# Another order of score tiles, maxima and values in two attention layers

## The chip, the core and the metric

The kernel runs on one core of a Trainium2 chip. The metric is device time in microseconds: the median of three runs, 6107.12 us for the kernel before (6103.73 to 6114.92). One more execution was taken with the hardware profiler; all views below come from that one.

The engines are called by the names of the profile: PE is TensorE, with PEld for its loads of the stationary operand, DVE is VectorE, ACT is ScalarE, POOL is GpSimd, and SP is SyncE, which here only issues DMAs. PSUM is the memory that matmuls write to. [...]

## The reference, cut to what matters

Four layers follow each other. Each is an attention over a context and a feed-forward part, and each part gets the layer-normed tokens and adds its result to them. There are 1024 tokens and 6404 context rows, 128 wide. The two layers that the change touches (1 and 3) have 16 heads of 8 and a softmax over the keys:

```python
scores = jnp.einsum('bhqd,bhkd->bhqk', q, k) * HEAD_DIM ** (-0.5)
attn = jax.nn.softmax(scores, axis=-1)
out = jnp.einsum('bhqk,bhkd->bhqd', attn, v)
```

So for every head and query the kernel needs the largest score, the exponentials of score minus maximum, their products with the values, and their sum.

## The kernel before

`attn_softmax` computes one of these two layers. It works in 16 units. A unit is a pair of heads (p and p + 8, called g = 0 and 1) and one half of the queries (512). The 6404 keys make 51 blocks of 128, the last one short; a unit therefore has 102 score blocks (key block c, head g), each of 128 keys by 512 queries.

Three kinds of work are woven into one stream, and they are named by letters:

- **S** (lines 1205 to 1223) fills a score tile and takes its exponential. The two heads lie in the two 64-row halves of the array (33 rows each are used: eight numbers four times over, as high and low parts, and a row that brings in the negative maximum). Score tiles alternate in form. An x tile has two PSUM banks and takes two score blocks; a y tile has one bank and takes one. PE fills it (line 1218), and ACT writes the Exp to SBUF as px or py (line 1223). There is one x tile and one y tile in PSUM (lines 1069 and 1070); the SBUF tiles px and py have three buffers each.
- **M** (`more_max`, line 1091, and `max_group`, line 976) computes approximate scores for 128 queries and 512 keys in bf16, one matmul for each head (line 990), and DVE takes their maxima (line 994). The PSUM tile, `pair_ps`, has two buffers. 52 such groups belong to a unit, and they are those of the next unit: the maxima run 8 groups ahead of it. The last group of a unit is followed by `max_found` (line 1023) and two steps later by `max_to_rows` (line 1029), which transposes the maxima on PE and adds them into the query operand qS.
- **P** (`values`, line 1104) multiplies the exponentials of one pair of key blocks (four score blocks) with the values; four matmuls of 32 columns each stand side by side in the array (line 1108), and the result adds up in one PSUM bank, `o_ps`, over the unit.

The loop over the pairs of key blocks has 26 steps in a unit. What a step issues, and in which order, stands in a tuple of strings, and step i takes string i % 3; i begins at 0 in each unit:

```python
order = ("SMSMSP", "SMSMP", "SMSMSP")
```

From there `tc.manual_schedule` (line 1076) makes PE, ACT and DVE issue in exactly this order; each engine waits where an operand or a buffer isn't ready. P takes the pair of the step before (`waiting`, line 1231). S does nothing when the unit's 102 score blocks are gone, and M does nothing when all maxima of the layer are done. Behind each step line 1232 makes one more M if the maxima have fallen behind.

When P has worked off a unit's last pair, `finish` (line 1153) starts a chain: `out_of_banks` copies o_ps to `ob` on ACT and sends the denominators through DRAM to spread them; three steps later `inverted` inverts them on DVE; six steps later `normalized` brings them into all rows with a matmul (line 1140) and multiplies on DVE (line 1141); seven steps later `projected` multiplies with the output weights (line 1147) and adds to the tokens (line 1151); eight steps later the DMAs for the queries of unit u + 2, and the keys of pair p + 2, are issued (`loads`, line 1173). These jobs are put behind the step that is due, and those that need PSUM take a buffer of `pair_ps` in turn with M.

In unit 15 no maxima are left. The buffers of `pair_ps` are given back, and each M of the strings takes a piece of other work instead (lines 1202 and 1204): in layer 1 the keys of layer 2, and in both layers, from step 9 on, the first half of the experts.

## Time and profile before

| What | us |
|---|---|
| median of three runs | 6107.12 |
| the profiled execution | 6117.12 |
| its span (first to last instruction) | 6115.4 |
| layer 1's units (first values 1099.6, last output copy 2310.9) | 1211 |
| layer 3's units (first values 4785.6, last output copy 6007.0) | 1221 |
| one undisturbed unit (output copies at 1249.88 and 1320.32) | 70.44 |
| PE, DVE, ACT busy between 1500 and 1600 | 92.5, 85.5, 74.9 of 100 |

A line of a group names the source line, engine, operation, the tiles written and read, the shapes and the count; behind the first bar stand the busy time and the mean time of one in ns; behind the second the time the engine stood idle just before, and what released it. A line of the timeline has the start, the time it took, the engine and line, how many instructions were merged (x2), and in brackets the idle time before it with its releaser. A line of the waits names who waited for whom, with total, number and longest. A line of the windows has the stretch and its length, then the busy time and number of instructions of PE, PEld, DVE, ACT and POOL, then the granted clock of TensorE, the share of the DMA engines and GB/s. The starts of matmuls are exact; their ends are modelled, and they overlap in the array.

### The profile page before, as it was taken

The numbers are of one execution on the slowest core, as the hardware profiler recorded it, in microseconds if no ns is written. First come the engines' busy times: TensorE is split into PE (matmuls) and PEld (weight loads), VectorE is DVE, ScalarE is ACT, GpSimd is POOL, SyncE is SP. The second block draws the span as 40 slices with busy tenths as digits, with TensorE's granted clock in tenths as the row PEclk, the third lists the DMA queues.
The fourth block names the chain that finished last, engine by engine and source line by source line (L and its number), as shares of the span: only waits on it lengthen the run. The fifth ranks groups of instructions, "written<-read, shape, count | busy, mean of one in ns | idle before, by whom it ended". The sixth has DMA issues, their size and how long they took to land. (4 is left out here: it accounts for less than half of the span.)

```text
span 6115.4 us, 84274 instructions
## 1 busy us (share of the span) xinstructions
PE 5633.9 (92%) x33200; PEld 2168.9 (35%) x33408; DVE 4786.1 (78%) x5825; ACT 4225.9 (69%) x5284; POOL 965.7 (16%) x687
## 2 busy tenths in 40 slices
PE   6999988899999998999999988999997899999987
PEld 2333335333333345333333333333333333333334
DVE  5555535888888844999999899999998888888834
ACT  3555544677777775788888777788884677777764
POOL 4888883100000010000000000000002000000001
PEclk8999988899999998999999899999997899999978
DMA  0000011100111041000000000000002100011001
GB/s 18 3 2 3 1 48 51 31 14 14 16 18 17 4 151 44 13 13 14 13 14 14 11 11 11 11 15 13 15 10 65 33 14 14 14 16 19 7 16 40
DMA packets 139360, 130.46 MB, mean 21 GB/s; under 512 B 30749, under 2 KB 120277, under 8 KB 137982
## 3 DMA queue, kind: packets, MB, share of 16 engines
q1 hardware_dynamic: 129894, 103.35, 7.7%
q0 software_dynamic: 5296, 17.22, 0.9%
q8 instruction: 264, 4.33, 0.3%
q10 hardware_dynamic: 3760, 4.36, 0.2%
q14 instruction: 146, 1.20, 0.1%
HBM read 102.18 MB, written 35.85 MB: 23 GB/s over the span
## 5 line engine op out<-in xcount | busy, mean ns | idle before, releaser
L994 DVE TENSOR_REDUCE mx<-pair_ps 128x2 f32<-128x1024 f32 x1612 | 1810.2, 1176 | 249.5 <-PE pair_ps L990 228.6
L1223 ACT ACTIVATE px<-x_ps 128x1024 f32<-128x1024 f32 x1088 | 1114.4, 1024 | 313.1 <-PE x_ps L1218 306.5
L1612 DVE TENSOR_TENSOR e<-e,inv 128x1024 f32<-128x1024 f32 (+1 forms) x816 | 992.7, 1218 | 11.0 <-PE pair_ps L1452 0.9
L1108 PE MATMUL o_ps<-px,v 128*32 128x512 f32 x4352 | 905.4, 620 | 0.0
L1108 PE MATMUL o_ps<-py,v 128*32 128x512 f32 x2176 | 897.9, 618 | 0.0
L1461 ACT CAST lb<-pair_ps 128x1024 bf16<-128x1024 f32 (+1 forms) x714 | 720.5, 1009 | 250.8 <-PE pair_ps L1452 227.2
L990 PE MATMUL pair_ps<-kb,qz 64*128 64x512 bf16 (+1 forms) x3224 | 826.5, 386 | 54.0 <-DVE mx L994 37.6
L1223 ACT ACTIVATE py<-y_ps 128x512 f32<-128x512 f32 x1088 | 647.3, 595 | 326.2 <-PE y_ps L1218 320.6
L1555 ACT ACTIVATE e<-x_ps 128x1024 f32<-128x1024 f32 (+1 forms) x816 | 840.8, 1030 | 29.6 <-PE x_ps L1552 27.9
L1564 PE MATMUL s_ps<-e,ident 128*128 128x512 f32 (+1 forms) x1632 | 851.4, 604 | 0.4
L1218 PE MATMUL x_ps<-qS,kS 33*128 33x512 f32 x2176 | 713.9, 534 | 125.8 <-ACT px L1223 125.7
L400 POOL TENSOR_TENSOR acc<-acc,pt 128x1024 f32<-128x1024 f32 x256 | 602.3, 2353 | 65.3 <-ACT pt L389 51.0
L342 DVE TENSOR_REDUCE mx<-b_ps 128x2 f32<-128x1024 f32 (+1 forms) x306 | 341.2, 1115 | 345.2 <-PE b_ps L338 345.2
L1218 PE MATMUL y_ps<-qS,kS 33*128 33x512 f32 x1088 | 570.0, 524 | 7.3 <-ACT py L1223 7.3
L1620 PE MATMUL o_ps<-e,vz 128*32 128x256 f32 (+1 forms) x6528 | 537.0, 399 | 7.9 <-DVE e L1612 7.7
L1469 DVE TENSOR_TENSOR low<-lb,low 128x1024 bf16<-128x1024 bf16 (+1 forms) x714 | 487.1, 682 | 20.1 <-ACT lb L1461 20.0
L1552 PE MATMUL x_ps<-mneg,identb 128*128 128x512 bf16 x1424 | 453.4, 389 | 40.4 <-issue 32.8
L1548 PE MATMUL x_ps<-qS,kS 32*128 32x512 f32 x1632 | 478.4, 582 | 0.0
L389 ACT ACTIVATE pt<-x_ps,bias 128x1024 f32<-128x1024 f32 x288 | 305.6, 1111 | 213.9 <-PE x_ps L384 199.0
L1218 PEld LDWEIGHTS x_ps<-qS,kS 33*128 33x128 f32 x2176 | 286.2, 192 | 460.9 <-ACT px L1223 217.0
L990 PEld LDWEIGHTS <-qz 64*128 64x128 bf16 x3224 | 265.9, 95 | 340.5 <-issue 240.0
L1218 PEld LDWEIGHTS y_ps<-qS,kS 33*128 33x128 f32 x1088 | 207.2, 190 | 476.4 <-issue 242.1
(387 smaller groups left out, 6298.4 us busy)
## 6 DMA issues: line engine op xcount, KB each, us to landing
kS<-kst SPq DMA_DIRECT2D x400, 64.0 KB
kS<-kd SPq DMA_DIRECT2D x120, 200.1 KB
w<-in_L_ffn_w SPq DMA_DIRECT2D x48, 256.0 KB
kst<-kd POOLq DMA_DIRECT2D x24, 512.0 KB, 14.0
kd<-kh SPq DMA_DIRECT2D x12, 512.0 KB
kd<-k SPq DMA_DIRECT2D x12, 512.0 KB
qS<-qd SPq DMA_DIRECT2D x256, 16.0 KB
kb<-in_L_ffn_w SPq DMA_DIRECT2D x16, 256.0 KB
```

Of the source, the lines that this page charges most:

```text
L400: nc.gpsimd.tensor_tensor(accs[u][:n], first[:n], pt[:n], ALU.add)
L990: nc.tensor.matmul(m[:, g, :n], qzs[u][r, ts(t, P)], kb[r, at : at + n], start=True, stop=True,)
L994: nc.vector.tensor_reduce(mxs[u][:, t, b], m[:, :, :n], AX.X, ALU.max)
L1108: nc.tensor.matmul(o[32 * j : 32 * j + 32], v[:, c, ds(VW * h, 32)], pt, start=i == 0, stop=c + 2 >= NK,)
L1218: nc.tensor.matmul(s[:, k], kS[p % 2][r, ts(c, P)], qS[u % 2][r], start=True, stop=True,)
L1223: nc.scalar.activation(pt[:, : len(some)], s[:, : len(some)], AF.Exp)
L1461: nc.scalar.copy(t[:n], m[:n])
L1469: nc.vector.tensor_tensor(low[:n], t[:n], low[:n], ALU.min)
L1555: nc.scalar.activation(pair(i, k), s[:n], AF.Exp)
L1564: nc.tensor.matmul(firsts[i], self.ident[:n], es[i, h // 4][:n, h % 4], start=k == 0, stop=k == K - 1,)
L1612: nc.vector.tensor_tensor(e, e, r, ALU.mult)
L1620: nc.tensor.matmul(outs[half][32 * g : 32 * g + 32, cols], vz[i % 2][:n, ds(P * j + 32 * g, 32)], es[i, j][:n, g, cols], start=c == 0 and ...
```

## The change

One line changes. Layers 1 and 3 both use it. In a step, values now stand behind two filled score tiles and two sets of maxima in one string, behind three of each in the next, and behind two score tiles and one set of maxima in the third. The first string has one more score tile behind its values.

```diff
-            order = ("SMSMSP", "SMSMP", "SMSMSP")
+            order = ("MSMSPS", "MSMSMSP", "SMSP")
```

Over three steps both tuples have eight S, six M and three P. Everything else is the same: buffers, tiles, the jobs behind the steps and the steps they are due at. A unit's 26 steps are eight times the three strings and then the first two once more; these two have four M before and five after.

## The prediction

> **What bounds the kernel now.** I read the page's shares and slices first, then the groups, then the waits and the timeline of layer 1's steady stretch, last the granted clock of short windows. S stands for filling a score tile (line 1218; x holds two score blocks, y one), M for a set of maxima (lines 990, 994), P for a block of values (line 1108); "section" is what PE issues between two P. A step takes one turn of the loop over pairs of key blocks; three steps make a round.

> ```profile
> PE 5633.9 (92%) x33200; PEld 2168.9 (35%) x33408; DVE 4786.1 (78%) x5825; ACT 4225.9 (69%) x5284; POOL 965.7 (16%) x687
> ...
> L994 DVE TENSOR_REDUCE mx<-pair_ps 128x2 f32<-128x1024 f32 x1612 | 1810.2, 1176 | 249.5 <-PE pair_ps L990 228.6
> L1223 ACT ACTIVATE px<-x_ps 128x1024 f32<-128x1024 f32 x1088 | 1114.4, 1024 | 313.1 <-PE x_ps L1218 306.5
> ...
> L1223 ACT ACTIVATE py<-y_ps 128x512 f32<-128x512 f32 x1088 | 647.3, 595 | 326.2 <-PE y_ps L1218 320.6
> ```

> No engine is full in these layers: the Exps of ACT wait 306.5 and 320.6 us for scores, the maxima of DVE 228.6 us. The waits of 1300 to 2000 us (us in total, times, longest) show the circle, since PE waits for the same Exps:

> ```profile
> ACT py L1223 <- PE y_ps L1218: 101.1, 155, 4.0
> ACT px L1223 <- PE x_ps L1218: 84.9, 182, 1.4
> DVE mx L994 <- PE pair_ps L990: 71.2, 96, 1.6
> ...
> PE x_ps L1218 <- ACT px L1223: 38.6, 78, 0.7
> ```

> There is one x tile and one y tile in PSUM, so an x can be refilled only after its Exp. One section of the timeline on PE, then ACT beside it:

> ```profile
> 1511.63 0.51 PE L1218 MATMUL x_ps<-qS,kS 33*128 33x512 f32 x2
> 1511.98 0.39 PE L990 MATMUL pair_ps<-kb,qz 64*128 64x512 bf16 x2
> 1512.02 0.58 PE L1218 MATMUL y_ps<-qS,kS 33*128 33x512 f32 x1
> 1512.35 0.48 PE L990 MATMUL pair_ps<-kb,qz 64*128 64x512 bf16 x2
> 1513.32 0.51 PE L1218 MATMUL x_ps<-qS,kS 33*128 33x512 f32 x2 [0.48 <-ACT px L1223]
> 1513.75 0.62 PE L1108 MATMUL o_ps<-py,v 128*32 128x512 f32 x1
> ...
> 1514.75 0.49 PE L1218 MATMUL y_ps<-qS,kS 33*128 33x512 f32 x1
> ```
> ```profile
> 1512.24 1.02 ACT L1223 ACTIVATE px<-x_ps 128x1024 f32<-128x1024 f32 x1 [0.63 <-PE x_ps L1218]
> 1513.16 0.59 ACT L1223 ACTIVATE py<-y_ps 128x512 f32<-128x512 f32 x1
> 1513.92 1.02 ACT L1223 ACTIVATE px<-x_ps 128x1024 f32<-128x1024 f32 x1 [0.17 <-PE x_ps L1218]
> ```

> This section is S M S M S with an x at both ends. From x to x: 0.60 to the Exp, 1.02 of Exp, 0.06 to the refill, 1.68 us; PE has nothing it may issue in the meantime. The three sections take 2.12, 1.13 and 1.60 (the last waits 0.4 for py), the P 1.00 each (1513.75 to 1514.75, 0.996 unrounded): **7.83 a round**, as repeated starts show (reduces at 1499.84, 1507.68, 1515.51).

> **The change, part by part.** It adds and removes no instruction: a round keeps 8 S, 6 M, 3 P. The DMAs of a unit hang on step numbers, so on SP and POOL nothing is moved past anything; the qz that POOL writes is wanted a whole unit later.

> *The round.* The new sections are: first M x M y; second x M y M x M y; third x M y. No wait is taken away; the two x that must lie 1.68 apart now have M y M between them, and y M follows. Rows for one matmul deep work: y M x M, 1506.92 to 1508.04, four matmuls in one half of the array, 1.13 with 0.07 of waiting; so about 0.24 each.
> - Second: x at 0, x again at 1.68, M; y must wait for the y before: its Exp starts at 0.60+1.02-0.10 = 1.52 (the next Exp starts 0.10 before the recorded end of the one before) and ends at 2.12, so y at 2.17, and P 0.41 behind a y: 2.58.
> - Third: x M y, one matmul less than 1.13: 0.89. Its x wants the Exp of the x at 1.68, over at 3.31; the section starts at 3.58. Free.
> - First: M x M y: the four of 1.13 without the wait and with the shorter load first, 1.02. Its x wants an Exp over at 5.21, issued at 5.5 or later. Free. Its own Exp ends at 7.2, before the next second section at 7.48.
> - Sum: 2.58 + 0.89 + 1.02 + 2.99 = **7.48**, 0.35 less than 7.83.

> DVE must follow: a reduce starts 0.43 behind its M, the next 1.13 later (two took 2.35, 1.22 + 1.13), and an M waits for the reduce two before. Reduces start at 0.77, 1.90, 3.04, 4.35, 5.9, 7.02 and again at 8.25: six need 6.8 of 7.48. M five waits to 2.06 and was due at 2.03. Hidden, with 0.6 to spare; if the cover went, the round could not fall below 6.8 anyhow.

> *The end of a unit.* 26 steps are 8 rounds and two steps. The second of these has one score block left and becomes x M y M M P: the third M waits for the first's reduce (over at 1.99), P at 2.36, and the next unit's second M waits 0.47 for DVE. The two steps cost 2.02 + 3.36 + 0.47 = 5.85; before 3.11 + 1.87 = 4.98 (P starts 1173.35, 1175.21). +0.85.

> *Work hung on steps.* The denominators' matmul (line 1140: 1194.99 to 1196.04) and the projection (1147: 1198.27 to 1199.36) cost 1.16 and 1.08 now. Line 1140 comes at the end of a first step: before behind P, now behind x, inside the second section. Its slot in the two M buffers makes the fourth M wait for the product on DVE (0.69, 1.22 behind the matmul, over at 2.33) and the fifth for a reduce over at 3.46, so P comes at 4.06 instead of 2.58: 1.48. Projection 1.09. The transposed maxima (0.58 now): 0.58 to 0.95, taken 0.8. Together +0.55.

> [...]

> *Unit:* 8 x (-0.35) + 0.85 + 0.55 = **-1.4 us of 70.44** (output copies at 1249.88 and 1320.32). Bounds: the sections of 0.89 and 1.02 by their issue times alone would be 0.81 and 0.93, round 7.31, unit -2.8; with 0.1 more each, 7.68 and +0.2. I keep the middle, nearest to the measured 1.13.

> *The slots.* The two left-over steps have 5 M instead of 4, so a unit has 53 for 52 groups. The maxima run ahead and end in step 14 of unit 14 instead of 21, leaving eleven steps there with S and P alone. At full clock these take about 7.17 a round by the same chain (ACT sets it), and unit 14 would take 66 instead of 69.5. But the clock:

> ```profile
> 1405.40:1408.80 3.40, 2.92 (x17) 0.82 (x14) 2.35 (x2) 2.46 (x3) 0.00 (x0) 1.00 0.50 60
> 1408.80:1415.60 6.80, 6.80 (x29) 3.35 (x28) 3.73 (x4) 1.62 (x2) 0.00 (x0) 0.50 0.51 63
> ...
> 5840.60:5853.00 12.40, 10.21 (x64) 3.23 (x62) 0.81 (x2) 9.09 (x12) 0.00 (x0) 1.00 0.00 0
> 5853.00:5904.00 51.00, 47.90 (x154) 15.35 (x152) 7.62 (x32) 23.21 (x31) 3.54 (x3) 0.50 0.01 1
> ```

> In layer 3 the granted clock (first number behind the brackets) fell to 0.50 twelve us after the last M and stayed, rounds of 11.6 (P at 5856.1 and 5867.8). Some six of the eleven steps at that pace cost 6.5 x (11.6-7.2)/3 = 10 us: unit 14 becomes +6. [...]

> *Sum.* Per layer thirteen whole units -18, unit 0 (its first nine steps wait for keys) -1, unit 14 +6; unit 15, with expert work in place of M, 0: -13, both layers **-27**. The profiled execution took 6117.1 (span 6115.4) and becomes 6090; the median shown is 6107.1, ten lower, and becomes **6080**.

> **The rivals.**
> 1. *More:* the short round of 7.31 and the clock staying up in unit 14: 27 units x 1.4 + 20 = 58 more, 6022. For: issue times 0.35 and 0.04 between S, M and y. Against: the four matmuls' 1.13.
> 2. *No change:* the round is 7.6, by 0.06 in each of the sections that I could not read off. A unit then gains 0.4, both layers 11, and unit 14's tails take 12 back: 6108. For: such short sections do not occur in the trace. Against: the same walk gives 7.83 for the old order.
> 3. *Slower, by the clock:* the window before a fall at 1408.8 holds line 1140 and half a section's waiting. Now that matmul is followed by two waits inside one section of 4.06, longer than the 3.4 us before that fall. A fall costs 1.5 or 2.9 us (units of 71.95 and 73.36 against 70.44); nine units of both layers have one, 21 us in all. If nearly all 28 whole units fall, 19 more at 2.4 are +45: 6125. It decides from 11 more falls on (27/2.4).
> 4. *It does not do what it says:* the strings put two, three and two score tiles before P in a step, but one S stands behind P in the first step, so that between P lie 2, 4 and 2. The walk is of that order: 6080, as forecast.

> **How the numbers follow.** Forecast (6045 to 6094) 0.42; rival 1 0.22; rival 2 0.17; rival 3 0.19. About 0.2% (12 us) is what a measurement of this kernel can tell from no change: faster 0.64, same 0.17, slower 0.19. The range goes from rival 1's 6022 to 6130, past rival 3.

> **What would show it.** Reduces of equal place 7.48 apart; PE waiting for px once a round, in the second section alone; output copies 69 apart; maxima of a unit found ever earlier; clock 0.50 in the tail of unit 14 of both layers. Rounds of 7.83 or more, or waits of M for DVE in ordinary rounds, make it wrong; so do more than some twenty falls of the clock.

## The result, and the profile after

The changed kernel takes 6112.04 us (median of 22 runs, 6097.79 to 6124.68) against 6099.34 us for the kernel before on the same chip (22 runs, 6089.27 to 6121.13): a ratio of 1.0021, with a 95% interval of 1.0013 to 1.0028. It is 12.7 us slower, where 27 us less were forecast. The profiled execution took 6121.45 us, its span 6119.7, 4.3 us more than that of the kernel before.

The page of the changed kernel, the same groups as before:

```profile
PE 5651.8 (92%) x33408; PEld 2085.3 (34%) x33408; DVE 4800.3 (78%) x5825; ACT 4214.1 (69%) x5284; POOL 965.2 (16%) x687
...
L994 DVE TENSOR_REDUCE mx<-pair_ps 128x2 f32<-128x1024 f32 x1612 | 1827.6, 1177 | 173.5 <-PE pair_ps L990 152.8
L1223 ACT ACTIVATE px<-x_ps 128x1024 f32<-128x1024 f32 x1088 | 1113.7, 1024 | 595.6 <-PE x_ps L1218 592.9
...
L1223 ACT ACTIVATE py<-y_ps 128x512 f32<-128x512 f32 x1088 | 645.1, 593 | 53.2 <-PE y_ps L1218 42.4
```

The waits were moved, and a few got less. ACT now waits 592.9 us ahead of x tiles and 42.4 ahead of y tiles (306.5 and 320.6 before); DVE waits 152.8 us for maxima's scores in place of 228.6. The waits of 1300 to 2000 us say the same:

```profile
ACT px L1223 <- PE x_ps L1218: 171.7, 326, 4.1
...
DVE mx L994 <- PE pair_ps L990: 45.3, 105, 1.6
PE x_ps L1218 <- ACT px L1223: 30.1, 63, 0.7
PE pair_ps L990 <- DVE mx L994: 19.7, 35, 1.3
```

PE's wait for px is down from 38.6 us (78 times) to 30.1 (63 times). The second section of a round on PE, up to the P behind it:

```profile
1497.21 0.49 PE L1218 MATMUL x_ps<-qS,kS 33*128 33x512 f32 x2
1497.55 0.39 PE L990 MATMUL pair_ps<-kb,qz 64*128 64x512 bf16 x2
1497.59 0.58 PE L1218 MATMUL y_ps<-qS,kS 33*128 33x512 f32 x1
1498.05 0.39 PE L990 MATMUL pair_ps<-kb,qz 64*128 64x512 bf16 x2
1498.88 0.50 PE L1218 MATMUL x_ps<-qS,kS 33*128 33x512 f32 x2 [0.44 <-ACT px L1223]
1499.26 0.39 PE L990 MATMUL pair_ps<-kb,qz 64*128 64x512 bf16 x2
1499.37 0.49 PE L1218 MATMUL y_ps<-qS,kS 33*128 33x512 f32 x1
1499.79 0.62 PE L1108 MATMUL o_ps<-px,v 128*32 128x512 f32 x2
```

From x to x 1.67 us (1.68 forecast), to P 2.58 (2.58). Reduces of equal place start at 1495.64 and 1503.11, 7.47 apart. The round is what the forecast said, and a unit without disturbance takes 68.9 to 69.3 us. The time is lost elsewhere. The layers cut by output copies, in the two profiled executions (units 1 to 13 are thirteen units together):

| us, before / after | layer 1 | layer 3 |
|---|---|---|
| units 1 to 13 | 930.6 / 916.8 | 922.3 / 920.1 |
| unit 14 | 69.5 / 74.8 | 70.5 / 75.4 |
| unit 15 | 131.3 / 141.0 | 151.9 / 151.5 |
| time at half clock in units 1 to 13 | 34.1 / 34.1 | 13.7 / 41.0 |
| starts of such a fall, both layers | 9 before | 14 after |

A fall of the clock in unit 1 of the changed kernel, and the one in the tail of its unit 14, in windows (the first number behind the brackets is the granted clock):

```profile
1198.60:1202.00 3.40, 2.60 (x12) 0.81 (x12) 2.55 (x4) 2.52 (x3) 0.00 (x0) 1.00 0.01 2
1202.00:1205.40 3.40, 3.40 (x16) 1.68 (x16) 1.73 (x2) 0.72 (x2) 0.00 (x0) 0.51 0.02 5
...
2140.70:2150.90 10.20, 8.84 (x53) 2.92 (x53) 0.69 (x1) 8.31 (x12) 0.00 (x0) 1.00 0.00 0
2150.90:2171.40 20.50, 19.75 (x69) 4.82 (x69) 0.00 (x0) 10.68 (x15) 0.00 (x0) 0.50 0.00 1
```

All 14 falls in units 1 to 13 of the changed kernel start 18.6 to 19.9 us behind the unit's start (that is, the output copy of the unit before), behind line 1140 (2.8 to 4.1 us behind its start). All nine of the kernel before start 16.6 to 17.0 us behind it, behind the same line (0.9 to 1.5 us). The granted clock of both profiles is 1.00 or 0.50 and nothing else. All falls of one profile, 42 before and 51 after, begin within 0.01 us of a common grid of 3.413 us (1202.05, 1341.99 and 1481.94 after are 41 steps apart) and last 3.41, 6.83, 10.24 us and so on, but for the one in which the profile ends. This makes a sharp test: each unit has one grid point in such a stretch. Before, every grid point that lay at 16.6 to 17.0 us brought a fall (9 of 9), and none of the 17 at other places (15.0 to 18.4). After, every one at 18.6 to 19.3 did (12 of 12), 2 of the 13 at 19.6 to 20.0, and not the one at 20.6. Where the grid lies against a unit differs from unit to unit and from profile to profile (the first falls start at 63.98 us before and at 61.99 after, 1.99 us apart, which is no whole step); the new order has the wider place to be hit. How wide, the run e1_ends below shows, whose units 1 to 13 have the same strings: every grid point at 18.1 to 19.6 us brought a fall (12 of 12). That is 1.5 us, against at most 0.8 before (no fall at 16.45 and at 17.22). In the kernel before, 29 runs of one comparison go from 6084.8 us at a mean clock of 0.964 to 6118.1 at 0.956, with a correlation of -0.97, so the spread between executions is the clock's too. And the falls are not those of one profile: all 22 runs of the changed kernel have a mean clock of 0.949 to 0.955, below the 0.956 to 0.964 of those 29 (the tail of unit 14 counts in it too).

PE was mostly busy ahead of the two falls shown: 2.60 of the 3.40 us ahead of the one in unit 1, and 8.84 of the 10.20 us ahead of the one in the tail of unit 14.

### The profile page after: what moved, and what is told of

The parts are those of the page before. It is cut to its first block, busy times and chain, and to the rows that moved or that the text cites. A ratio compares the mean times of both kernels' runs of the same rounds, so it can differ in the third digit from the quotient of the medians.

```text
span 6119.7 us, 84478 instructions
## 1 busy us (share of the span) xinstructions
PE 5651.8 (92%) x33408; PEld 2085.3 (34%) x33408; DVE 4800.3 (78%) x5825; ACT 4214.1 (69%) x5284; POOL 965.2 (16%) x687
## 3 DMA queue, kind: packets, MB, share of 16 engines
q0 software_dynamic: 5296, 17.22, 0.9%
## 5 line engine op out<-in xcount | busy, mean ns | idle before, releaser
L994 DVE TENSOR_REDUCE mx<-pair_ps 128x2 f32<-128x1024 f32 x1612 | 1827.6, 1177 | 173.5 <-PE pair_ps L990 152.8
L1223 ACT ACTIVATE px<-x_ps 128x1024 f32<-128x1024 f32 x1088 | 1113.7, 1024 | 595.6 <-PE x_ps L1218 592.9
L1612 DVE TENSOR_TENSOR e<-e,inv 128x1024 f32<-128x1024 f32 (+1 forms) x816 | 992.8, 1218 | 11.0 <-PE pair_ps L1452 0.9
L1108 PE MATMUL o_ps<-px,v 128*32 128x512 f32 x4352 | 929.7, 636 | 0.0
L1108 PE MATMUL o_ps<-py,v 128*32 128x512 f32 x2176 | 920.7, 630 | 0.0
L990 PE MATMUL pair_ps<-kb,qz 64*128 64x512 bf16 (+1 forms) x3224 | 636.3, 385 | 100.8 <-DVE mx L994 80.5
L1223 ACT ACTIVATE py<-y_ps 128x512 f32<-128x512 f32 x1088 | 645.1, 593 | 53.2 <-PE y_ps L1218 42.4
L1218 PE MATMUL x_ps<-qS,kS 33*128 33x512 f32 x2176 | 586.1, 528 | 101.8 <-ACT px L1223 101.8
L1218 PE MATMUL y_ps<-qS,kS 33*128 33x512 f32 x1088 | 620.7, 570 | 3.9 <-ACT py L1223 3.8
L1552 PE MATMUL x_ps<-mneg,identb 128*128 128x512 bf16 x1632 | 501.3, 389 | 7.6 <-DVE mneg L1474 7.6
L1469 DVE TENSOR_TENSOR low<-lb,low 128x1024 bf16<-128x1024 bf16 (+1 forms) x714 | 487.1, 682 | 19.9 <-ACT lb L1461 19.7
L1218 PEld LDWEIGHTS x_ps<-qS,kS 33*128 33x128 f32 x2176 | 217.6, 191 | 643.2 <-ACT px L1223 511.0
L990 PEld LDWEIGHTS <-qz 64*128 64x128 bf16 x3224 | 176.9, 94 | 640.6 <-issue 587.6
L1452 PE MATMUL pair_ps<-qn,kb 32*128 32x512 bf16 (+1 forms) x1632 | 319.5, 388 | 44.0 <-ACT lb L1461 21.2
```

Source lines behind the costliest of these rows:

```text
L990: nc.tensor.matmul(m[:, g, :n], qzs[u][r, ts(t, P)], kb[r, at : at + n], start=True, stop=True,)
L994: nc.vector.tensor_reduce(mxs[u][:, t, b], m[:, :, :n], AX.X, ALU.max)
L1108: nc.tensor.matmul(o[32 * j : 32 * j + 32], v[:, c, ds(VW * h, 32)], pt, start=i == 0, stop=c + 2 >= NK,)
L1218: nc.tensor.matmul(s[:, k], kS[p % 2][r, ts(c, P)], qS[u % 2][r], start=True, stop=True,)
L1223: nc.scalar.activation(pt[:, : len(some)], s[:, : len(some)], AF.Exp)
L1552: nc.tensor.matmul(s[:, t], self.identb, mnegs[i], start=False, stop=True)
```

## The experiments

Theory A: the short round is real; what takes it back are the falls at line 1140, the 53rd slot for maxima (line 1091's groups run ahead, and unit 14 ends in steps without them) and the two units at the ends. Rivals: the falls alone (B); or the order is slower on ordinary executions, whatever the profile shows (C). Each ratio is against the kernel before on the same chip. "Falls" are those in units 1 to 13 of the profiled execution: us at half clock in layers 1 and 3, and how far behind the unit's start they begin.

| kernel | us | ratio (95%) | falls | where |
|---|---|---|---|---|
| before | | 1 | 34.1, 13.7 | 16.6 to 17.0 |
| changed | 6112.0 | 1.0021 (1.0013 to 1.0028) | 34.1, 41.0 | 18.6 to 19.9 |
| e1_ends | 6106.7 | 1.0004 (0.9992 to 1.0017) | 37.5, 30.7 | 18.1 to 19.9, one at 10.2 |
| e2_slots | 6089.0 | 0.9983 (0.9968 to 0.9998) | 34.1, 64.9 | 17.4 to 20.8, five at 10.5 to 11.0 |
| e3_late | 6097.6 | 0.9991 (0.9979 to 1.0002) | 6.8, 20.5 | 19.5 to 19.8, one at 10.6 |
| e4_all | 6026.1 | 0.9868 (0.9851 to 0.9886) | 6.8, 0 | 11.5 |
| e5_slots_late | 6054.1 | 0.9914 (0.9896 to 0.9932) | 34.1, 13.7 | 10.5 to 11.6 |
| e6_rows | 6074.6 | 0.9947 (0.9929 to 0.9965) | 6.8, 0 | 10.7 |
| e7_before_late | 6085.9 | 0.9964 (0.9950 to 0.9978) | 0, 0 | |
| e8_nine | 6119.0 | 1.0018 (1.0006 to 1.0029) | 30.7, 30.7 | 25.8 to 27.0, one at 11.1 |
| e9_before_rows | 6072.7 | 0.9961 (0.9946 to 0.9976) | 0, 0 | |
| e10_slots_rows | 6042.4 | 0.9911 (0.9895 to 0.9927) | 0, 27.3 | 10.8 to 11.3 |
| e11_first | 6038.4 | 0.9907 (0.9890 to 0.9923) | 6.8, 0 | 11.9 |
| e12_last | 6047.3 | 0.9921 (0.9907 to 0.9936) | 20.5, 0 | 10.7, 11.0, 20.3 |
| e13_rows_last | 6073.3 | 0.9953 (0.9936 to 0.9971) | 0, 0 | |
| e14_slots_rows_last | 6049.4 | 0.9906 (0.9882 to 0.9930) | 13.7, 34.1 | 10.3 to 10.7 |
| e15_slots_rows_ends | 6030.6 | 0.9885 (0.9866 to 0.9905) | 6.8, 6.8 | 11.5, 12.0 |
| e16_slots_rows_again | 6037.9 | 0.9890 (0.9869 to 0.9910) | 27.3, 13.7 | 10.4 to 11.5 |
| e17_second | 6037.9 | 0.9880 (0.9860 to 0.9901) | 13.7, 10.2 | 19.4 to 21.5 |
| e18_all_second | 6025.3 | 0.9867 (0.9845 to 0.9890) | 10.2, 20.5 | 19.4 to 21.7 |

### One cause each, and all together

**Old strings in units 0 and 15** (e1_ends):

```diff
+            usual = ("SMSMSP", "SMSMP", "SMSMSP")
-                    for what in order[i % 3]:
+                    strings = usual if u in (0, UNITS - 1) else order
+                    for what in strings[i % 3]:
```

> Units 0 and 15 of both layers go back to the old strings, units 1 to 14 keep the new ones. Theory A (the loss sits in places of its own, besides the units that run evenly): in the profiled pair unit 0 lost 3.5 and 4.1 us and unit 15 of layer 1 lost 9.7 us, so this run should be some 17 us below the changed kernel, 6095 us or 0.999 of the kernel before. Theory B (the loss is the clock's falls at line 1140 in units 1 to 13 alone, which this leaves as they are): no gain, 1.002 of the kernel before. Theory C (the shorter round of the profile isn't there on ordinary executions, and the new order is the slower one wherever it stands): two of sixteen units go back, so at most 2 us of the 13 come back, 1.0015 to 1.002.

1.0004: 10 us come back, between A and B. With this interval and that of the changed kernel it is clear of none of the three.

**52 slots** (e2_slots):

```diff
-                    for what in order[i % 3]:
+                    for what in "MSMSP" if i == STEPS - 1 else order[i % 3]:
```

> Step 25 gets its own string MSMSP, so that a unit has 52 slots for maxima, not 53: the surplus no longer runs ahead, the steps around a unit's end lose one M, and the steps without maxima at the end of unit 14 become fewer. Theory A: 0.85 us at 28 unit ends is 24 us less, and the ends of unit 14, which lost 5.3 and 4.9 us in the profiled pair, give these back: some 34 us below the changed kernel, 6078 us or 0.9965 of the kernel before. Theory B (the clock's falls at line 1140 decide; what a unit's end saves in work is taken back by more falls): 6105 to 6112 us, 1.001 to 1.002. Theory C (order slower everywhere): 1.002.

0.9983: 23 us below the changed kernel, where A said 34. Units without a fall went from 69.2 to 68.0 us and unit 14 from 74.8 and 75.4 to 70.4 and 68.4, as forecast; but the falls of layer 3 rose from 41.0 to 64.9 us in the profiled execution. A is the nearer; of B it has that falls take back a part.

**Line 1140 a step later** (e3_late):

```diff
-                for i, f in ((3, second), (6, third), (7, fourth)):
+                for i, f in ((3, second), (7, third), (8, fourth)):
-                later.setdefault(at + 8, []).append(loads)
+                later.setdefault(at + 9, []).append(loads)
```

> Line 1140 comes one step later (7 steps after a unit's end), line 1147 8 steps after, the loads 9 steps after; nothing else is changed, so that the two-row matmul no longer stands in the stalled section where the changed kernel's clock falls to a half. Theory A: the falls in units 1 to 13 cost 19 us and 22 us in the profiled execution (15 and 6 before the change); without them 20 to 41 us less than the changed kernel, 6071 to 6092 us, 0.9955 to 0.999 of the kernel before, and a granted clock of 1.00 through units 1 to 13. Theory B (the same, and the only cause): at the lower end, 0.9955. Theory C (order slower everywhere, the falls are by the way): 1.001 to 1.002, falls or not. A rival to A within it (the clock falls wherever few rows stand, whichever step it is): the falls stay as many and move a step, 1.001 to 1.003.

0.9991, at A's upper end, and the falls went from 75.1 us to 27.3. Line 1140 now stands directly behind P, but behind the P of the section that waits 0.44 us for px, much as it stood in the kernel before (behind a wait of 0.48). All three falls left at this line start there, on neighbouring grid points (19.55, 19.66 and 19.77 us; none at 19.48 and 19.97). The profiled execution is the kernel's quickest (6084 of 6084 to 6120) and has a mean clock of 0.957, where the twelve runs go from 0.949 to 0.957, so others probably had more falls.

**The three together** (e4_all):

> The three edits together: old strings in units 0 and 15, 52 slots for maxima in units 1 to 14, line 1140 a step later. Theory A (three separate places, their prices add up): 17 + 34 + 20 to 41 us below the changed kernel, 6020 to 6041 us, 0.987 to 0.9905 of the kernel before. Theory B (only the clock at line 1140 counts): 0.9955 to 0.997. Theory C (order slower everywhere): 1.000 to 1.002.

0.9868, 77 us less than the kernel before beside it (6102.7) and A's lowest figure. It gives more than its parts (0.0017 + 0.0038 + 0.0030 below the changed kernel, against 0.0153): I read it so that falls take back what a shorter unit saves as long as they are there, as the rise in e2_slots suggests; no run isolates it. Theories B and C are out. Its page:

```profile
PE 5561.0 (92%) x33200; PEld 2080.5 (35%) x33408; DVE 4800.2 (80%) x5825; ACT 4206.8 (70%) x5284; POOL 965.7 (16%) x687
...
L994 DVE TENSOR_REDUCE mx<-pair_ps 128x2 f32<-128x1024 f32 x1612 | 1827.5, 1177 | 154.5 <-PE pair_ps L990 129.6
L1226 ACT ACTIVATE px<-x_ps 128x1024 f32<-128x1024 f32 x1088 | 1114.5, 1024 | 528.7 <-PE x_ps L1221 518.1
```

DVE is busy as long as in the changed kernel (4800). PE is busy 73 us less than in the kernel before (5633.9, with as many records): the same work, less of it at half clock (mean granted clock 0.961 and 0.956 in the two profiles).

### What it is about line 1140

**The same later place in the kernel before** (e7_before_late, the edit of e3_late):

> The kernel before with line 1140 a step later and nothing else. It has 52 slots already. Theory A (line 1140's place brings the falls in both orders): the falls of its units 1 to 13, 34 us and 14 us long and some 21 us in cost, go, and it runs at 0.9965 to 0.998. The round's own worth is then the distance from this kernel to the one with 52 slots and the later line 1140: by units of 70.45 and 68.0 us, 28 of them, 69 us or 0.011. Rival (the later place is only good for the new order, whose stalled section it was in): 0.999 to 1.001, or slower by new falls.

0.9964, no falls. So the kernel before paid for line 1140 too. The line now stands behind the P of its section without a wait. (The edit moves line 1147 and the loads as well; the runs with 128 rows below move nothing.) The other half of the expectation failed: from here to e5_slots_late, the new order with 52 slots and the later line, it is 0.0050 (30 us) and not 0.011; e5 still has 47.8 us of falls.

**Two steps more, in the same string again** (e8_nine):

```diff
+                for i, f in ((3, second), (9, third), (10, fourth)):
+                later.setdefault(at + 11, []).append(loads)
```

> The changed kernel with line 1140 9 steps after a unit's end in place of 6, line 1147 10 after, the loads 11 after: later than the kernel with 7, but back in the same string of the three, behind P and x. Theory A (it is the section that line 1140 stands in): the falls in units 1 to 13 stay, 30 to 45 us a layer, and the time at 1.001 to 1.003 of the kernel before. Rival (what helps is more distance from the unit's end and from its transfers): as the kernel with 7 or better, 0.998 to 0.9995, with falls of under 20 us a layer.

1.0018, falls of 30.7 us a layer, and they moved with the line: 25.8 to 27.0 us behind the unit's start, one round later than in the changed kernel. It is the section, not the distance. (In it unit 15's first half of the experts begins on tokens that lack unit 14's projection.)

**128 rows in place of 2** (e6_rows):

```diff
-                nc.tensor.matmul(m, sel, rr, start=True, stop=True)
+                nc.tensor.matmul(m, self.ident, ob, start=True, stop=True)
```

> The changed kernel with line 1140's matmul on 128 rows (identity by ob, the same 128 x 512 output in float32) in place of 2 rows; this leaves out the division by the sums. The same time on the engine, the same place in the same section, the same wait behind it. Theory A (few rows in a stalled section bring the clock down): the falls in units 1 to 13, 34 and 41 us long in the profile of the changed kernel, go to under 15 us a layer, and the time to 0.996 to 0.999 of the kernel before. Rival (the stall itself, with VectorE's answer behind line 1140, brings it down, whatever the rows): the falls stay, 1.001 to 1.003.

0.9947, 45 us less than the changed kernel, and none of the 26 grid points at 17.8 to 21.0 us brought a fall. The section itself is the same. First the changed kernel's, then this one's, with PE's matmul of line 1140 and the two M that wait behind it:

```profile
1198.43 1.12 PE L1140 MATMUL pair_ps<-rr,selr 2*128 2x512 f32 x2
...
1200.39 0.39 PE L990 MATMUL pair_ps<-kb,qz 64*128 64x512 bf16 x2 [0.29 <-DVE ob L1141]
...
1201.52 0.39 PE L990 MATMUL pair_ps<-kb,qz 64*128 64x512 bf16 x2 [0.51 <-DVE mx L994]
```
```profile
1890.76 1.13 PE L1140 MATMUL pair_ps<-ob,ident 128*128 128x512 f32 x2
...
1892.72 0.39 PE L990 MATMUL pair_ps<-kb,qz 64*128 64x512 bf16 x2 [0.29 <-DVE ob L1141]
...
1893.85 0.39 PE L990 MATMUL pair_ps<-kb,qz 64*128 64x512 bf16 x2 [0.50 <-DVE mx L994]
```

The windows of the second, at the same place against the grid as 1198.60 to 1202.00 above (18.9 and 19.1 us behind the unit's start):

```profile
1890.70:1894.10 3.40, 2.61 (x14) 0.99 (x12) 2.53 (x4) 2.27 (x3) 0.00 (x0) 1.00 0.00 0
1894.10:1897.50 3.40, 3.40 (x28) 1.64 (x29) 2.88 (x4) 1.38 (x3) 0.00 (x0) 1.00 0.00 0
```

One more thing differs, and it is not the clock. Behind the last unit of a layer line 1140 waits for the denominators' DMA (rr from rd, 14.5 us in all in the changed kernel), and the matmul on `ob` waits for none. From the last output copy of layers 1 and 3 to the end of the projection it is 15.5 and 21.0 us in the changed kernel and 9.5 and 15.8 here. So some 11 of the 45 us come from there and some 34 are left; units 1 to 13 of the two profiles differ by 33.

**The same 128 rows in the kernel before** (e9_before_rows):

> The kernel before with line 1140 on 128 rows (identity by ob), as in the changed kernel's version with 128 rows; the division by the sums is left out. The two then differ in the order alone, with the falls at line 1140 out of both. Theory A: its falls in units 1 to 13 go (21 us in cost), 0.9955 to 0.9975 of the kernel before; the changed kernel's version, at 0.9947, is below it by what the units give (26 units at 1.3 us, 34 us) less what the ends of unit 14 and unit 15 take (10 to 25 us): a distance of 10 to 25 us, 0.0015 to 0.004. Rival (128 rows only help the new order; the order before loses nothing at line 1140): 0.999 to 1.001.

0.9961, no falls: with 128 rows the kernel before gains 24 us (15 to 33 by the interval), and the changed one 45 us (34 to 57). Here too some 11 us are those of the layers' ends (17.3 and 23.9 us become 11.2 and 18.7); units 1 to 13 of the two profiles differ by 20, and e7_before_late, which keeps that wait, gained 23. With line 1140's rows out of both the new order leads by 0.0014 only, a little under A's range. Units 1 to 13 of this kernel take 915.8 and 916.7 us.

### The 53rd slot, and unit 0 and unit 15

**52 slots and a later line 1140, new strings everywhere** (e5_slots_late, the edits of e2_slots and e3_late):

> The 52 slots and the later line 1140, with the new strings in units 0 and 15 too. What is asked is whether those two units lose anything of their own. Theory A2 (they don't: what looked like a loss in unit 15 was the clock coming down out of unit 14, and unit 0 differs between runs of one kernel as much as between the two orders): as the version with all three edits, 6020 to 6035 us, 0.987 to 0.989 of the kernel before. Rival (the old strings are better in those units, by 3.5, 4.1 and 9.7 us as the profiled pair had it): 17 us above the version with all three, 6043 us, 0.9895 to 0.991.

0.9914, above the figures of both, though the rival's lie in its interval; falls of 34.1 us in layer 1, at a new place.

**128 rows and 52 slots** (e10_slots_rows):

> The changed kernel with 52 slots and with line 1140 on 128 rows in its own place (the division by the sums is left out). With 52 slots and two rows the falls of units 1 to 13 were more than ever (34 and 65 us long). Theory A (they are line 1140's): under 15 us a layer and 0.987 to 0.990 of the kernel before. Rival (a shorter unit brings the clock down by itself, through less work in each 3.4 us): falls of over 30 us a layer stay, 0.9955 to 0.9985.

0.9911, between the two; no fall at line 1140, but four at 10.8 to 11.3 us in layer 3.

**Old strings in one of the two units** (e11_first and e12_last, with the edits of e5_slots_late):

> 52 slots, later line 1140, old strings in unit 0 alone (unit 15 has the new ones). The version with the old strings in both units ran at 0.9868, the one with the new ones in both at 0.9914, and their profiles differ by 18 us in units 1 to 13 (falls of 7 and 0 us against 34 and 14 us) and by 9 us in the two units 15. Theory P (unit 0's string sets where the following units stand against the clock's steps of 3.41 us, of which 20 make 68.27 us, close to a unit's 68.0, so that a fall comes back unit after unit or never): falls of units 1 to 13 under 15 us a layer, 0.988 to 0.9895. Rival (it is unit 15's string): 0.9905 to 0.992.

> 52 slots, later line 1140, old strings in unit 15 alone (unit 0 has the new ones). Theory P (unit 0's string sets the falls of units 1 to 13, unit 15's gives 9 us in the two layers): falls of units 1 to 13 as with the new strings in both, 14 to 35 us a layer, and 0.989 to 0.9905. Rival (it is unit 15's string): 0.9865 to 0.988.

0.9907 and 0.9921. The falls went as theory P has it in layer 1 (one with the old strings in unit 0, three without); in layer 3 neither has any. The times did not: e11 lies in its rival's range, e12 above both of its own. Theory P is not shown.

**With line 1140's falls out** (e13_rows_last, e14_slots_rows_last, e15_slots_rows_ends, e16_slots_rows_again, together on one chip):

> The changed kernel with line 1140 on 128 rows (the division by the sums is left out) and the old strings in unit 15; 53 slots. Theory U (unit 15's new strings cost some 5 us in layer 1 and up to 13 in layer 3, by the profiles of the two versions with 128 rows: 136.9 and 151.5 us against 131.7 and 138.5): 10 to 18 us below the version with new strings everywhere (0.9947): 0.9918 to 0.9931. Rival (unit 15 is long because the clock comes down in the tail of unit 14, before it, whatever its strings): 0.994 to 0.9955.

> 128 rows, 52 slots, old strings in unit 15. Theory U: 6 to 15 us below the version with 52 slots and new strings everywhere that runs beside it. Rival (the tail of unit 14, which 52 slots take away): within 4 us of it.

> 128 rows, 52 slots, old strings in units 0 and 15. Theory P (unit 0's string only moves the units against the clock's steps, which matters only through line 1140's two rows): within 4 us of the version with the old strings in unit 15 alone. Rival (unit 0's string is worth something of its own, by the 3 to 4 us of the first comparison of profiles, in each layer): 6 to 8 us below it.

> 128 rows, 52 slots, new strings everywhere, beside the other three as their base: 0.9895 to 0.9927 of the kernel before, as the first time.

e13, at 0.9953, is where the rival has it; e14 is 11.5 us above e16 and fits neither; e16, at 0.9890, is a little under its range, and the same kernel had 0.9911 on another chip (e10). e13 to e16 is the slot alone but for unit 15: 6073.3 to 6037.9, 35 us, where 24 at units' ends and 10 in the tails were expected. Unit 15's strings alone (e13 against e6, e14 against e16) make no difference that these runs can tell. The profiles can: unit 15 of layer 1 takes 128.7 to 133.0 us in the ten with the old strings there and 133.4 to 141.0 in the ten with the new ones (means 130.9 and 135.7); with 52 slots as with 53; in layer 3 the means are 145.8 and 149.6, and the two groups overlap. Unit 0 ends at the same time with either (means 1178.8 and 1179.2 us in layer 1). e15 is 19 us below e14, neither "within 4" nor the rival's 6 to 8: the units of 68.0 us still have falls, 13.6 us of them in the profile of e15 and 47.8 in that of e14. That unit 0 decides how many is not shown.

### A second place

In e14_slots_rows_last the falls lie 10.3 to 10.7 us behind the unit's start. There stands the inversion of the denominators (lines 1130 and 1131), put behind step 3. DVE and PE of one such section, then its windows:

```profile
5313.21 0.17 DVE L1130 TENSOR_TENSOR dr<-dr 128x8 f32<-128x8 f32 x1 [0.63 <-DMA dr<-dd]
5313.41 0.20 DVE L1131 RECIPROCAL dr<-dr 128x8 f32<-128x8 f32 x1
```
```profile
5313.46 0.49 PE L1221 MATMUL x_ps<-qS,kS 33*128 33x512 f32 x2 [0.44 <-ACT px L1226]
5314.76 0.61 PE L990 MATMUL pair_ps<-kb,qz 64*128 64x512 bf16 x2 [0.80 <-DVE mx L994]
```
```profile
5311.30:5314.70 3.40, 2.22 (x17) 0.76 (x10) 2.73 (x6) 2.87 (x5) 0.00 (x0) 1.00 0.04 4
5314.70:5321.50 6.80, 6.74 (x28) 1.65 (x27) 3.49 (x4) 2.50 (x4) 0.00 (x0) 0.50 0.66 87
```

DVE waits 0.63 us for the denominators' DMA, the reduce behind it is late, and M waits 0.80 in the section that has waited 0.44 for px already. So the job was put a step later:

```diff
-                for i, f in ((3, second), (7, third), (8, fourth)):
+                for i, f in ((4, second), (7, third), (8, fourth)):
```

> 52 slots, line 1140 a step later (7), and the inversion of the denominators a step later too (4 in place of 3); new strings in all units. Theory S (the falls 10.3 to 12.0 us behind a unit's output copy are those of the inversion's wait for its DMA in the stalled section): no falls there, under 7 us of falls a layer in units 1 to 13, and 0.986 to 0.9885 of the kernel before, against 0.9914 without this edit. Rival (a unit of 68.0 us has falls somewhere whatever stands there): 14 us or more a layer, 0.990 to 0.992.

> The same with the old strings in units 0 and 15, the version that ran at 0.9868 with the inversion at 3. Theory S with P (unit 0's string matters only by which units meet a fall): within 6 us of the version beside it, whose units have no falls left to be moved. Rival (the old strings are worth something in these two units): 10 us or more below it. Against 0.9868 little is left to gain: 0.985 to 0.9875.

e17: 0.9880 against 0.9914, and none of 26 grid points at 9.8 to 12.9 us brings a fall. So the place is shown by the falls: in e5_slots_late, with the inversion a step earlier, seven start there. By the times it is not, since the intervals of e17 and e5 overlap. Under 7 us of falls a layer were expected, and 13.7 and 10.2 are left, now at line 1140's later place. e18 is at 0.9867 with 30.7 us of falls, 12.6 us below e17 as the rival has it, with intervals that overlap; in the two profiles 6 us of that are unit 15. e4 and e18 are the quickest versions, 1.3% below the kernel before.

## Why the prediction was wrong, point by point

1. **The round, right.** 7.47 to 7.48 us measured. P stand 3.58, 1.89 and 2.01 us apart (3.58, 1.89 and 2.02 from the sections). Rivals 1 and 2 are out. The 35 waits of M for the maxima's buffer between 1300 and 2000 all stand at work hung on steps or at a unit's end, none in an ordinary round. There is some luck in the two short sections: the 0.24 for a matmul is not a quarter of 1.13 less 0.07 (0.265), and they came out to 0.01 all the same.
2. **The unit, right.** With the clock held up, thirteen units take 899.8 and 900.4 us with the new order (e13) and 915.8 and 916.7 with the old (e9): -32.3 in both layers, against -36 from -1.4 a unit. The +0.85 at a unit's end has the right sign and about the right size: without the 53rd slot a unit takes 68.0 us in place of 69.2. In the changed kernel P follows the one before by 5.05 us where line 1140 stands (4.06 + 1.00 forecast).
3. **The step that failed: work hung on steps.** "Line 1140 ... now behind x, inside the second section" was priced at 1.48 us of waiting and no more. The waiting was right (point 2); the clock was left to rival 3, and the forecast took the falls of before as they were. The runs with 128 rows gain 24 us in the kernel before and 45 us in the changed one. Some 11 us of each arise at the layers' ends, where a DMA is no longer waited for, so that the falls cost some 13 and 34 us (20 and 37 in units 1 to 13 of the profiles, against e9 and e13). Some +21 us belonged into the sum, known to about 15 by the intervals; the profiles say +16. Rival 3 had the line and the place. Its measure was wrong: it let the forecast turn from 11 more falls on, and five more (14 against 9), at the greater length, were enough together with unit 15 (point 5).
4. **The slots, right.** Unit 14 +5.3 and +4.9 us against +6, from the clock in its tail, which fell 14.7 and 14.9 us behind the start of the last M. Rival 1's 20 us, for a clock that stays up there, no run shows: in the changed kernel 0.50 was granted for 20.5 us of that tail in both layers (from 2150.95 and from 5840.76). The surplus is worth more without it than the prediction could use: 35 us for a string of five letters.
5. **Unit 15, wrong: 0** against +4.8 us in layer 1 and about +4 in layer 3 (means of the profiles; the times of e13 and e14 don't show it). Here other work takes the letters' places, and I had walked only the stream of S, M and P. Which wait in unit 15 makes the difference was not taken apart.
6. **Unit 0, right within its size:** -1 against 0 (its end in layer 1, 1178.8 and 1179.2 us).

From the measured sizes: -32 + 21 + 10 + 9 = +8 us; 12.7 were measured. Some 5 stay unassigned, less than the +21 can be off by.

## What to carry to other kernels

A matmul can cost more than its duration. Line 1140 took 1.1 us here, with 2 rows as with 128, and with 2 rows the falls behind it cost some 13 us in the kernel before and 34 us in the changed one (point 3): look where such a line stands. Here the clock fell where it stood in a section that waits (0.29 and 0.51 us, the changed kernel) or behind one (0.48 in the kernel before, 0.44 for what is left in e3), and not where it stood behind a section without a wait (e7). Compare the granted clock of short windows at every line that a reordering moves. When a shorter loop gives less than its walk says, look for time at half clock before doubting the walk; here the same reordering comes to +0.2%, or with three small edits around it to -1.3%. Of that 0.4% is the later line 1140, which the kernel before could have had without the new order (e7).

## What the runs showed that I had not expected

- Two stretches with equal busy time (2.60 and 2.61 of 3.40 us) and equal waits, with line 1140 (1.1 us) on 2 rows in one and on 128 in the other, were followed by a granted clock of 0.51 and 1.00.
- Whether a fall comes is a matter of at most 0.8 us (the kernel before) or some 1.5 us (the new strings) in where the unit stands on a grid of 3.413 us. A unit of 68.0 us is close to 20 such steps (68.27), so a hit or a miss can repeat: in e14 falls start at 5174.8, 5314.7, 5454.7 and 5594.6, 41 steps or two units apart (one of them lengthened by the fall).
- Three edits that gave 10, 23 and 18 us by themselves (0.0017, 0.0038 and 0.0030) gave 93 us together.
